# Routing without a sort: rows go to each expert's next place in DRAM, and answers come back by groups

## The chip, the cores and the metric

The kernel runs on one core of a Trainium2 chip. Its engines work side by side and wait for one another through semaphores: TensorE (PE in the profile; its weight loads are PEld), VectorE (DVE), ScalarE (ACT), GpSimd (POOL) and SyncE (SP). Every engine runs its own instructions in order. DMAs are issued from the queues of SP, ACT and POOL and share the core's 16 DMA engines. The metric is device time in microseconds of one execution.

## The reference

A four-layer model over x of 2048 tokens (2 x 1024) and 256 columns. Each layer adds a gated cross attention to a small context (64 rows a batch) and a gated feed-forward part to x. What matters here:

- Layer 0's feed-forward part is a mixture of 8 experts, two for each token, of hidden size 1024, with a capacity.
- Layer 1's feed-forward part has causal self-attention (16 heads of 16, 4 key heads) and then a mixture of 8 experts of hidden size 512, one for each token:

```python
x = x + out @ Wo + bo
h2 = rmsnorm(x, ln2_w)
logits = h2 @ Wr + br
top1 = jnp.argmax(logits, axis=-1).reshape(-1)
u = jnp.einsum('td,edf->tef', xt, W1) + b1
u1, u2 = (u[..., :HID], u[..., HID:])
act = u1 * jax.nn.sigmoid(u2)
y_all = jnp.einsum('teh,ehd->ted', act, W2) + b2
y = jnp.take_along_axis(y_all, top1[:, None, None], axis=1)[:, 0, :]
return x + y.reshape(batch, seq, DIM)
```

- Layer 2 is cross attention and a quantised product, layer 3 cross attention and a mixture of 16 experts. They are not changed, but layer 2's cross attention is the first reader of layer 1's answers.

## The kernel before, in words

The 2048 tokens are 16 row tiles of 128 (`NT`), four to a group of 512 (`NG` = 4 groups). x stays in SBUF for the whole run. TensorE's order is written out by hand (`manual_schedule`); on the other engines, and on the DMA queues, a planner orders the work at build time by its own estimates, and the chip then keeps that order.

*Layer 0's end* (`l0`). Each expert's rows are gathered from DRAM, worked on, and its answers scattered into `ybuf` (`scattered`, L1395, on POOL). When all are written (`wrote`), eight loads of 512 KB (L844, on SP, four buffers) bring them back, and 32 VectorE operations (L854) add them to x, for all four groups. Layer 1 begins after that.

*Cross attention* (`ctx_attn`, shared by layers 1 and 2). It works through the 16 row tiles. `norm` of a group (statistics on VectorE, the reciprocal root on POOL, scaling on ACT), `turn` and `project` give a group's queries. `norm(0)` and `norm(1)` stand before the loop, `norm(2)` and `norm(3)` in its steps 2 and 6. Layer 1's projection and norms for its self-attention (`l1_front`) run in the same loop as `then` steps.

*Self-attention* (`l1_attention`). For each of 16 query tiles: `scores`, exponentials and `values` in blocks, with the maxima for a tile two ahead (`greatest`); `place` writes the maxima into the queries by a POOL DMA (`qT<-mT`, L1210). Finished tiles queue their routing steps in `routing`: the gate (L1281), the output projection (L1290), `normed` (L1308, which also writes the normalised row to `hbuf` through SP, L1309), `turned` and `chosen` (L1325, the logits and the choice, a one-hot `oh`). They are queued four tiles at a time, so the last four tiles' steps run after the loop.

*Layer 1's experts* (`l1_experts`, L1552). All eight experts' weights are loaded by SP (L1564, L1568: 8 MB and 4 MB) into two tiles, while `sort_tiles` (L1429) turns the one-hots into a list for each tile of 128 rows of one expert: which rows to gather (`gi`), where their answers go (`si`) and which expert it is (`ei`). There are up to 23 tiles (`NS`); 19 always run, the last four under an `If`. For each tile POOL gathers the rows (`xg`, L1580) and the expert's biases spread over 128 partitions (`bt`, L1586, 640 KB), TensorE transposes the rows, multiplies (`up`, L1613, in two halves, `down`, L1633) with weights picked by a register, VectorE adds the biases (L1617, L1638), and POOL scatters the answers to the tokens' places. When all are written, four loads (L1670) bring them back and 16 operations add them to x (L236). Layer 2 begins after that, its loads behind these on SP.

## Time and profile before

| | us |
|---|---|
| median of 7 runs (2180.38 to 2190.69) | 2187.36 |
| the profiled execution | 2188.95 |
| its span | 2187.2 |
| busy: PE / DVE / ACT / POOL | 1849.0 / 1115.5 / 840.0 / 425.7 |
| layer 0's last answer on VectorE, first projection of layer 1 | 395.9, 428.8 |
| attention's last matmul, first matmul of the expert tiles | 981.5, 1032.1 |
| last answer of layer 1's experts, first projection of layer 2 | 1163.6, 1195.9 |

The profile is one execution. Its times start at the first instruction. A busy share says how long an engine worked in a stretch and not what held it when it did not; for that the view of the chain names what ended last at each step ("SPq" is the SP queue issuing a DMA, "issue" is time in which nothing that the profile shows was waited for). The granted clock is TensorE's as the throttle left it, 1.00 being full. In the timeline the start of a pipelined matmul is firm and its end modelled, so a step is read from start to start.

### The profile page before, as it was taken

The numbers are of one execution on the slowest core, as the hardware profiler recorded it, in microseconds if no ns is written. First come the engines' busy times: TensorE is split into PE (matmuls) and PEld (weight loads), VectorE is DVE, ScalarE is ACT, GpSimd is POOL, SyncE is SP. The second block draws the span as 40 slices with busy tenths as digits, with TensorE's granted clock in tenths as the row PEclk, the third lists the DMA queues.
The fourth block names the chain that finished last, engine by engine and source line by source line (L and its number), as shares of the span: only waits on it lengthen the run. The fifth ranks groups of instructions, "written<-read, shape, count | busy, mean of one in ns | idle before, by whom it ended". The sixth has DMA issues, their size and how long they took to land.

```text
span 2187.2 us, 26241 instructions
## 1 busy us (share of the span) xinstructions
PE 1849.0 (85%) x9627; PEld 1165.9 (53%) x9627; DVE 1115.5 (51%) x2437; ACT 840.0 (38%) x1603; POOL 425.7 (19%) x652
## 2 busy tenths in 40 slices
PE   7849999599778998993894978799999899998884
PEld 3437777377545455542553664455555555555563
DVE  5660010556677647722345763356662466655434
ACT  3402222354434564571112653354442454441121
POOL 1013331201421031113332133000000000000462
PEclk8969999799889999996997978799999999998997
DMA  4032331300000000006432200000000000002224
GB/s 145 20 110 88 118 118 62 115 1 1 7 2 2 1 11 2 11 11 252 158 141 84 97 1 0 0 1 1 1 1 0 1 1 1 1 1 87 61 89 155
DMA packets 70603, 107.09 MB, mean 49 GB/s; under 512 B 13779, under 2 KB 55382, under 8 KB 70214
## 3 DMA queue, kind: packets, MB, share of 16 engines
q1 hardware_dynamic: 54582, 63.17, 8.7%
q0 software_dynamic: 13824, 40.55, 5.5%
q8 instruction: 81, 1.33, 0.2%
q10 hardware_dynamic: 2064, 1.62, 0.2%
q14 instruction: 52, 0.43, 0.1%
HBM read 80.90 MB, written 24.15 MB: 48 GB/s over the span
## 4 chain that ended last, share of the span: by engine, by line
PE 49%; DVE 10%; issue 6%; ACT 6%; POOL 5%; DMA 3%; SPq 2%; another core or an unknown queue 0%; ACTq 0%; POOLq 0%; DVEq 0%
PE s L1910 6%; PE et L1933 4%; PE po L1945 4%; PE s L1174 3%; PE po L1244 3%; PE prj L204 3%; PE sT L1225 3%; PE po L352 3%; DVE nm L1180 2%; DVE nm L1918 2%; PE h L2084 1%; PE v L1840 1%; SPq L1568 1%; PE wo L2012 1%; PE s L548 1%
## 5 line engine op out<-in xcount | busy, mean ns | idle before, releaser
L1180 DVE TENSOR_REDUCE nm<-s 128x1 f32<-128x512 f32 (+3 forms) x304 | 184.0, 655 | 68.6 <-PE s L1179 46.7
L1920 ACT ACTIVATE e<-s,nm 128x1024 f32<-128x1024 f32 x128 | 141.4, 1110 | 180.2 <-DVE nm L1919 104.0
L1918 DVE TENSOR_REDUCE nm<-s 128x1 f32<-128x1024 f32 x128 | 150.9, 1219 | 97.6 <-PE s L1910 97.6
L1233 ACT ACTIVATE eT<-sT 128x512 f32<-128x512 f32 x288 | 148.8, 603 | 112.3 <-PE sT L1225 81.4
L1910 PE MATMUL s<-kT,qT 64*128 64x512 f32 x512 | 162.0, 635 | 11.1 <-ACT e L1920 11.1
L1933 PE MATMUL et<-ident,e 128*128 128x128 f32 x1024 | 140.8, 285 | 16.7 <-DVE eT L112 12.4
L1174 PE MATMUL s<-kT,qT 128*128 128x512 f32 (+3 forms) x384 | 129.4, 417 | 16.4 <-ACT qT L114 9.6
L1933 PEld LDWEIGHTS et<-ident,e 128*128 128x128 f32 x1024 | 114.4, 144 | 53.6 <-issue 22.2
L1945 PE MATMUL po<-eT,v 128*64 128x256 f32 x1024 | 125.6, 385 | 0.3 <-DVE eT L112 0.2
L1174 PEld LDWEIGHTS s<-kT,qT 128*128 128x128 f32 x384 | 73.1, 196 | 81.7 <-DVE nm L1180 27.1
L783 PE MATMUL h<-xeT,w 128*128 128x384 f32 (+1 forms) x416 | 108.9, 420 | 0.6 <-PEq L836 0.3
L112 DVE COPY eT<-et 128x512 f32<-128x512 f32 x128 | 87.8, 686 | 41.9 <-PE et L1933 39.9
L1945 PEld LDWEIGHTS po<-eT,v 128*64 128x64 f32 x1024 | 68.5, 136 | 69.4 <-issue 32.3
L787 ACT ACTIVATE hT<-h,b 128x384 f32<-128x384 f32 (+1 forms) x104 | 52.6, 508 | 137.5 <-PE h L783 120.8
L1957 POOL TENSOR_TENSOR ec<-scs,nm 128x1024 f32<-128x1024 f32 x8 | 15.2, 1901 | 461.4 <-DVE nm L1919 415.5
L793 DVE TENSOR_TENSOR y<-yp,b 128x256 f32<-128x256 f32 (+1 forms) x34 | 14.4, 422 | 177.3 <-PE yp L801 176.7
L801 PE MATMUL yp<-w,hT 128*128 128x256 f32 x464 | 102.8, 380 | 0.0
L1225 PE MATMUL sT<-qT,kT 128*128 128x512 f32 x288 | 96.9, 451 | 2.1 <-DMA qT<-mT 2.1
L1910 PEld LDWEIGHTS s<-kT,qT 64*128 64x128 f32 x512 | 58.5, 189 | 71.8 <-ACT e L1920 35.8
L801 PEld LDWEIGHTS yp<-w,hT 128*128 128x128 f32 x464 | 87.7, 190 | 15.5 <-issue 2.1
L1613 PE MATMUL up<-w,xT 128*128 x152 | 77.2, 632 | 15.2 <-DMA w<-in_L_ffn_W_dram 7.3
L783 PEld LDWEIGHTS h<-xeT,w 128*128 128x128 f32 x416 | 70.5, 191 | 35.4 <-issue 3.4
(495 smaller groups left out, 3580.1 us busy)
## 6 DMA issues: line engine op xcount, KB each, us to landing
w<-in_L_ffn_W_dram SPq DMA_DIRECT2D x24, 1024.0 KB
y<-ybuf SPq DMA_DIRECT2D x20, 512.0 KB
ybuf<-zero POOLq DMA_DIRECT2D x8, 512.0 KB
hbuf<-xn SPq DMA_DIRECT2D x32, 128.0 KB
w<-in_L_ffn_W_dram SPq DMA_DIRECT2D x8, 512.0 KB
x<-in_x_dram SPq DMA_DIRECT2D x16, 128.0 KB
hbuf<-hn SPq DMA_DIRECT2D x16, 128.0 KB
L_ffn_w1T<-in_L_ffn_w1T_dram SPq DMA_DIRECT2D x1, 2048.0 KB
```

The lines of the kernel that those rows point to most:

```text
L112: self.nc.vector.tensor_copy(out, in_)
L783: nc.tensor.matmul(p[:, :m], W[e][0][:, k, ts(hc, P)], X[e][:, k, r : r + m], start=k == 0, stop=k == DC - 1,)
L801: nc.tensor.matmul(p[:m, :D], hT[:, hc, r : r + m], W[e][1][:, hc, :], start=hc == 0, stop=hc == HC - 1,)
L1174: nc.tensor.matmul(o, qT[:, h0 + j, :], kT[:, (h0 + j) // 4, b * S + k0 : b * S + k0 + m], start=True, stop=k0 + m < n,)
L1180: nc.vector.tensor_reduce(nm[:, u, h0 : h0 + nh], s[:, : nh * m].rearrange("p (h k) -> p h k", h=nh), AX.X, ALU.max, negate=True,)
L1225: nc.tensor.matmul(s, kT[:, kv, b * S + kt * P : b * S + (kt + 1) * P], qT[:, 4 * kv : 4 * kv + 4, :], start=True, stop=kt < qt,)
L1233: nc.scalar.activation(eT[:, kv, :], s, AF.Exp)
L1910: nc.tensor.matmul(s[h][:, ts(u, 512)], qT[r, c, ts(2 * g + t, P)], kT[r, c, ts(u, 512)], start=True, stop=True,)
L1918: nc.vector.tensor_reduce(m, s[h], AX.X, ALU.max, negate=True)
L1920: nc.scalar.activation(e[n][h], s[h], AF.Exp, bias=m, accum_out=q["rs"][:, t, j])
L1933: nc.tensor.transpose(p[:, ts(j, P)], e[n][h][:, ts(k + j, P)], self.ident)
L1945: nc.tensor.matmul(po[j][64 * h : 64 * h + 64, :256], v[:, k, ts(2 * c + h, D3X)], eT[j][h][:, k, :], start=k == 0, stop=k == KM - 1,)
```

## The change

- Layer 1's sort goes. Every expert owns T rows of a DRAM buffer `xs1`. While attention still runs, `sent` counts a routed group's one-hots (two small matmuls), keeps a running row number for each expert in `bases`, and scatters each normalised row (POOL) to its expert's next row. The buffer's 17.8 MB are cleared beforehand: 68 DMAs of 256 KB on SP, five to a step of layer 1's cross attention.
- Routing is queued in groups of 4, 4, 4, 2, 1 and 1 row tiles; in the last two query tiles two steps are taken at a time, and a step waits until its tile's output has been turned.
- A tile of 128 rows is now a plain block of `xs1`. `tile_table` computes each tile's expert and first row; registers read from the table address three SP loads for each tile: its rows, its expert's W1 (1 MB) and its W2 (512 KB), four buffers each, three tiles ahead.
- Biases enter as matmuls: all experts' biases lie split into three bf16 parts in `bias1`, and a one-hot column `sel` of the tile's expert picks them (`biased`).
- A tile's answers overwrite its block (a POOL DMA with a register address). A token's answer is gathered by its row number (`slot`).
- The answers of layers 0 and 1 are no longer taken at the layer's end: `take(g)` is called by the next cross attention ahead of `norm(g)`. Layer 1's and layer 2's cross-attention pools release space tile by tile.

The diff, cut:

```diff
+NS1 = NT + E1 - 1
+R1 = T * E1 + 8 * P
     def ctx_attn(..., some=None, then=(), take=None):
-        qT, norm, turn, project = queries
+        qT, ready, turn, project = queries
+        def norm(g):
+            take(g)
+            ready(g)
     def l1_xattn(self, then, scratch, take):
-        with self.tc.tile_pool(name="l1x", bufs=1) as pool:
+        with self.tc.tile_pool(name="l1x", bufs=1, reuse_waits="tile") as pool:
...
             kbd, vblk = self.ctx_kv(pool, wk, wv)
+            scratch(pool)
     def l0(self, back):
-            for g in range(NG):
-                for u in range(2):
-                    y4 = pool.tile([P, 4, D], F32, tag="y4", name="y4", bufs=4)
+        def take(g):
+            for u in range(2):
+                y4 = back.tile([P, 4, D], F32, tag="y4", name="y4", bufs=2)
...
     def l1(self, take, taken, back):
+            def scratch(q):
+                row = q.tile([E1, 2 * H1 + D], F32, tag="brow1", name="brow1")
+                self.nc.sync.dma_start(out=row, in_=self.a["L1_ffn_b12"])
+                self.bias_rows(None, row, 2 * H1 + D, None, E1, d["bias"])
+                zero = q.tile([P, 512], F32, tag="zero1", name="zero1")
+                self.nc.gpsimd.memset(zero, 0.0)
+                flat = d["x"].rearrange("r d -> (r d)").rearrange("(k p f) -> k p f", p=P, f=512)
+                clear.extend(
+                    partial(self.nc.sync.dma_start, out=flat[k], in_=zero) for k in range(flat.shape[0])
+                )
+            def cleared(i):
+                if i > 0:
+                    for _ in range(5):
+                        if clear:
+                            self.after(clear.pop()(), self.first[-1:])
...
     def l1_attention(self, u, front, rest, front_done, ln2, d):
+            def sent(i, n):
+                v = nc.vector
+                q = oh[i].rearrange("p i e -> p (i e)")
+                m = n * E1
+                p = self.ps("count")
+                nc.tensor.matmul(p[:, m : 2 * m], self.ones, q, start=True, stop=True)
+                nc.tensor.matmul(p[:, :m], upper, q, start=True, stop=True)
+                within = p[:, :m].rearrange("p (i e) -> p i e", e=E1)
+                total = p[:, m : 2 * m].rearrange("p (i e) -> p i e", e=E1)
+                v.tensor_copy(bases[:, 0, :], bases[:, 4, :])
+                for j in range(n):
+                    o = bases[:, j + 1 if j + 1 < n else 4, :] if i + n < NT else d["next"]
+                    v.tensor_tensor(o, bases[:, j, :], total[:, j, :], ALU.add)
+                at = ap.tile([P, n, E1], F32, tag=f"at{n}", name="at")
+                v.tensor_tensor(at, within, bases[:, :n, :], ALU.add)
+                v.tensor_tensor(at, at, oh[i], ALU.mult)
+                row = ap.tile([P, 4], F32, tag="row", name="row", bufs=2)[:, :n]
+                v.tensor_reduce(row, at, AX.X, ALU.add)
+                v.tensor_copy(d["slot"][:, i : i + n], row)
+                for j in range(n):
+                    self.scattered(d["x"][:, :], d["slot"][:, i + j : i + j + 1], hn[i + j], d["put"])
...
+            few = {3: 4, 7: 4, 11: 4, 13: 2, 14: 1, 15: 1}
...
-                        if routing and (not tail or len(routing) > 9):
-                            routing.pop(0)()
+                        for _ in range(1 + (i > 13)):
+                            if routing and routing[0][0] in turned_back and (not tail or len(routing) > 9):
+                                routing.pop(0)[1]()
     def l1_experts(self, ln2, d, way):
+            self.tile_table(pool, d["next"], table, used)
+            sel = pool.tile([P, NS], BF16, tag="sel", name="sel")
+            nc.vector.tensor_scalar(sel, table[:, :, 0], d["p32"], None, ALU.is_equal)
...
+            def gather(s):
+                e = nc.values_load(table[0:1, s, 0:1], engines=[E.SP], min_val=0, max_val=E1 - 1)
+                r = nc.values_load(table[0:1, s, 1:2], engines=[E.SP, E.Pool], min_val=0, max_val=R1 - P)
+                xg = pool.tile([P, D], F32, tag="xg", name="xg", bufs=4)
+                ins = nc.sync.dma_start(out=xg, in_=d["x"][bass.ds(r, P), :])
+                own(ins.ins, wrote)
+                self.after(ins, d["put"])
+                read.append(ins.ins)
+                w1 = pool.tile([P, DC, 2 * H1], F32, tag="w1", name="w1", bufs=4)
                 nc.sync.dma_start(
+                    out=w1, in_=a["L1_ffn_W1"][bass.ds(e, 1)].rearrange("e (k p) h -> p (e k) h", p=P)
+                )
+                w2 = pool.tile([P, FC, D], F32, tag="w2", name="w2", bufs=4)
...
+            def biased(s, out, cols):
+                nc.tensor.matmul(
+                    out, sel[:, s : s + 1].to_broadcast([P, P]), d["bias"][:, cols], start=True, stop=False
+                )
             def up(s, w):
-                    reg[s] = nc.tensor.value_load(ei[0:1, s : s + 1], min_val=0, max_val=E1 - 1)
...
+                biased(s, p[:, h], h)
                 for k in range(DC):
+                    nc.tensor.matmul(p[:, h], xT[s][:, k, :], w1[:, k, h], start=False, stop=k == DC - 1)
-                nc.vector.tensor_tensor(u[:, h], p[:, h], bt[:, h], ALU.add)
                 if w:
-                    nc.scalar.activation(u[:, h], u[:, h], AF.Sigmoid)
+                    nc.scalar.activation(u[:, h], p[:, h], AF.Sigmoid)
                 else:
-                    nc.vector.tensor_tensor(u[:, h], u[:, h], u[:, H1:], ALU.mult)
+                    nc.vector.tensor_tensor(u[:, h], p[:, h], u[:, H1:], ALU.mult)
...
-                nc.vector.tensor_tensor(yo, y[:, :D], G[s][2][:, 2 * H1 :], ALU.add)
-                self.scattered(ybuf[:, :], si[:, s : s + 1], yo, wrote)
+                nc.vector.tensor_copy(yo, y[:, :D])
+                ins = nc.gpsimd.dma_start(out=ybuf[bass.ds(r, P), :], in_=yo).ins
+                own(ins, wrote + read)
+                wrote.append(ins)
...
+        def take(g):
+            for i in range(4 * g, 4 * g + 4):
+                y = way.tile([P, D], F32, tag="back", name="back", bufs=8)
                 self.after(
+                    nc.gpsimd.indirect_dma_start(
+                        out=y, out_offset=None, in_=ybuf[:, :],
+                        in_offset=bass.IndirectOffsetOnAxis(ap=slot[:, i : i + 1], axis=0),
                     ),
                     wrote,
                 )
+                self.add_gated(i, y, 5)
```

## The prediction, made before the result was known

> **What bounds the kernel now.** I read three views in this order: busy time by stretch, to find the stages in which TensorE is not full; the chain that ended last, to see what those stretches wait for; and the timeline of one expert tile, to see what TensorE pays for a tile.
>
> Busy time by stretch (start and end, length, busy time of PE, PEld, DVE, ACT and POOL with instruction counts, granted clock, DMA share, GB/s):
>
> ```profile
> 395.00:420.00 25.00, 0.40 (x2) 0.00 (x0) 16.30 (x45) 10.76 (x12) 3.96 (x10) 0.57 0.74 217
> 420.00:435.00 15.00, 12.50 (x36) 7.62 (x38) 12.76 (x49) 6.28 (x13) 8.38 (x14) 0.69 0.13 38
> ...
> 940.00:982.00 42.00, 41.42 (x246) 19.97 (x242) 5.14 (x15) 35.40 (x76) 9.64 (x16) 1.00 0.04 14
> 982.00:1005.00 23.00, 14.24 (x56) 9.83 (x57) 5.67 (x19) 6.70 (x18) 9.68 (x21) 0.80 0.07 23
> 1005.00:1032.00 27.00, 2.22 (x22) 1.43 (x21) 10.71 (x53) 0.00 (x0) 8.69 (x9) 0.50 1.01 396
> ...
> 1049.00:1164.00 115.00, 107.76 (x392) 64.81 (x392) 47.13 (x86) 20.80 (x36) 43.62 (x45) 1.00 0.34 121
> 1164.00:1196.00 32.00, 6.36 (x27) 5.46 (x27) 19.80 (x64) 3.98 (x9) 6.78 (x13) 0.57 0.44 130
> ```
>
> TensorE is full in the attention loop (41.42 of 42 us) and nearly so over the expert tiles (107.76 of 115). It is empty in three gaps: after layer 0's experts (395 to 420), between routing and layer 1's experts (1005 to 1032, all 16 DMA engines full) and after those experts (1164 to 1196).
>
> The chain in order of time (start, length, what), over the last two gaps:
>
> ```profile
> 979.54 1.98 PE po L1244 x16
> ...
> 984.83 2.00 PE gate L1281 x4
> ...
> 999.92 3.17 PE lg L1325 x14
> ...
> 1018.77 8.81 SPq L1568
> ...
> 1039.34 9.31 DMA w<-in_L_ffn_W_dram
> ...
> 1049.11 1.97 PE y L1633 x8
> ...
> 1143.17 24.63 DMA bt<-in_L_ffn_b_dram,ei
> 1168.16 3.81 DMA y<-ybuf
> 1171.99 3.27 DVE x L236 x8
> ...
> 1177.18 6.17 DMA mi<-in_mask_dram
> ```
>
> Attention ends at 981.5, routing of the last four row tiles at 1004.4; then the load of all eight experts' weights carries the chain until 1049. Behind the experts, the answers' way through DRAM and layer 2's own loads, queued behind it on SP, carry it.
>
> One tile's TensorE work:
>
> ```profile
> 1070.21 1.88 PE L1613 MATMUL up<-w,xT 128*128 x4
> 1071.92 0.60 PE L1626 MATMUL at<-ident,ub 128*128 128x128 f32 x4
> 1072.88 1.98 PE L1613 MATMUL up<-w,xT 128*128 x4 [0.35 <-DVE ub L1617]
> 1074.70 0.38 PE L1597 MATMUL xt<-ident,xg 128*128 128x128 f32 x2
> 1074.91 1.89 PE L1633 MATMUL y<-w,aT 128*128 x8
> ```
>
> The next tile's first row starts at 1076.64: 6.43 us a tile, of which TensorE waits 0.35.
>
> **The change, part by part.** The sum is made against the profiled execution, 2188.95 us (span 2187.2 and 1.75 around it). That is 1.59 above the median of 2187.36, which I take off at the end.
>
> *Layer 0's answers by groups: -10.* Now VectorE's last answer is ready at 395.86, the last scatter has landed at 399.53 (the release of POOL's brow memset), eight loads of y go out from 398.77, 32 adds to x run until 417.26, and only then the norms that feed TensorE's first projection, at 428.83. After, two loads and eight adds stand before the first norm. But on SP's queue the loads that layer 1 needs now come first in the program; those into the right-hand pools cannot go before 399.53. Some 12 issues at 0.45 each put the first y load at 405, with 1.6 MB of weights ahead of its 1 MB; at the 217 to 313 GB/s of this stretch y lands by 410.5. Adds end at 412.3, statistics at 412.9, POOL's rsqrt and mean take 2.3 (as from 420.57 to 422.91), ACT's four scalings 2.07, transposes and copies 1.2: first projection at 418.5. If y went first the gain would be 16; if VectorE is held by the new bias split or SP is later still, 4. I take 10, by the row of 0.45 an issue.
>
> *Layer 1's cross attention carries more: +3.* 24 adds of 0.40 to 0.48 (11 us) move beside a stage where VectorE is busy 106.76 of 165.6 us: 0 if they fit, 11 if all stall; I take 1. 68 clears of 256 KB write 17.8 MB; layer 0's zeros wrote at 406 GB/s, so 44 us of a DMA that is idle here (share 0.01). 68 SP issues at 0.45 are 31 us of an empty queue; behind them wait the y loads of group 3, with three row tiles of slack. The split of the eight experts' biases is three casts and two subtractions of 1280 columns: scaled from 0.35 and 0.53 at 384 columns, about 7 us of VectorE, most of it while VectorE waits for y: I take 2, ends 0 and 7.
>
> *Attention loop: +6.* Rows are now routed in groups of 4, 4, 4, 2, 1, 1, so three tiles' routing moves from the tail into a loop where TensorE is full: gate 1.3, output projection 2.9 (0.98 a tile), transposes 1.3, logits 0.6: 6.1; the counting matmuls of `sent` add about 0.3 for each of six groups. 8 us, less some 2 of gaps. On POOL each group's scatters (1.0 each) and on VectorE its ten 0.2 us operations stand before `qT<-mT`, which TensorE waits for only 2.1 us in all now; the cover is a query tile of lead. If it fails at each group, six times 2 us.
>
> *From attention to the first expert tile: -25.5.* Now 981.54 to the first up matmul at 1032.11: 50.6. After, step by step for one row tile: to the gate 3.3 (981.54 to 984.83); gate 1.9; projection, residual and square 2.6; POOL 1.5 and 0.6; transposes, copies and logits 1.8; choice 1.6 (six of 0.2 with gaps); count 1.4 (as 1004.42 to 1005.80); place 1.2: the scatter starts near 997.4 and has landed 3.9 us later (as 1164.25 to 1168.16). Beside it the tile table, 21 VectorE operations, takes 4 us at 0.19 each. Then two register reads on SP, xg, 1 MB of W1 at the 409 GB/s of this load: 2.6 plus about 2 from issue to landing: 1006.5, 25 us after attention. Register reads by an engine have no row of their own; TensorE's read for each tile leaves no gap in the 6.43, and POOL's first gather starts 0.83 after its index is written: 0 to 0.83 each, I take 0.5. The page "DMA: Bandwidth & Descriptors" of the Trainium skill (Latency and other measured facts) gives a floor of about 0.6 us for a `tensor_load`, which I read as such a register read; by it the pair on SP would cost 1.2, and no run here shows it.
>
> *The expert tiles: +7.* Now from 1032.11 to the last answer at 1163.97: 131.9, with the first tiles stalled on W2. Each tile gains three bias matmuls, 512, 512 and 256 columns of bf16; two 512-column bias matmuls of cross attention take 0.43 in the chain, so 0.54 a tile: 6.97. VectorE loses a 0.69 add, which gives nothing, as the half-tile wait then stands behind ACT's 0.63 sigmoid. 19 tiles are 132.4; the first 8 us at clock 0.50 (1032 to 1040 now) cost 4, the last tile's end 2: 138.4. The page "TensorE: Matmul & The Clock Gate" (Part 1) says that about 3.4 us of sustained work lift the clock; by it the cold start would cost 1.7 instead of 4. The trace's 8 us decides. Each tile now also loads 1.57 MB of weights and 0.13 of rows and writes 0.13: 1.83 MB, 4.5 us at 409 GB/s and 5.2 at the 349 of the W2 stretch, under the 6.97 that hides it, with three tiles of prefetch. The cost of this term runs from -3 (bias matmuls in the 0.35 wait and a short cold start) to +15 (a stall of 0.4 a tile).
>
> *Layer 1's answers by groups: -12.4.* Now 32 us from the last answer (1163.55) to the first projection (1195.91), among it 16 adds, the mask's load and its 2 us on VectorE. After: the write lands 4.6 later as now; four indirect gathers at POOL's pace of 1.25 with 3.0 from the last issue to data: 11.4; add and statistics 1.1; POOL's rsqrt stands behind group 1's four gathers: 16.5; scalings, transposes, copies 3.5: 20. If POOL does the rsqrt first, 2 less; if mask and weights are not in by then, 5 more.
>
> Sum: -10 + 3 + 6 - 25.5 + 7 - 12.4 = -31.9: 2157.0, or **2156** against the median.
>
> **The rivals.**
> *The queues give the answers back* (2173). SP sends layer 1's loads ahead of y and POOL holds the norms: the first boundary gains 0, the third 5: 17 us less gain. For it: both queues run in order and y now stands last on SP. Against: eight loads and 32 adds become two and eight.
> *Attention pays* (2168). The six groups each delay `qT<-mT` by 2 us on POOL. For: POOL's waits are in order; against: POOL is busy 9.64 of 42 us.
> *Larger gain* (2142). y first (6 more), bias matmuls half hidden in the 0.35 wait and a shorter cold start (8 more).
> *Slower: the tile loop is bound by its loads* (2214 at 10 us a tile, 19 times 3.03 over 2156). Place: SP, two register reads and three loads a tile, waiting for buffers. It decides at 8.6 us a tile, where 19 times 1.65 eat the 31.9, that is at 213 GB/s. For it: W1 and W2 are fetched 19 times instead of 8, with 1 KB rows in W2. Against: 349 to 414 GB/s in the present load, from the same queue.
>
> **How the numbers follow.** Forecast 0.50, with its own range 2145 to 2168; queues 0.17, attention pays 0.08, larger gain 0.12, load-bound 0.13. The measurement tells 0.2% (4.4 us) from no change. The first, second, third and larger cases are faster, 0.87, less 0.03 for their upper ends; of the load-bound case 0.01 falls within 0.2%: faster 0.84, same 0.04, slower 0.12. The range 2134 to 2188 holds all but most of the load-bound case and the low end of the larger gain.
>
> **What would show it.** Right: first projection of layer 1 near 418, first up matmul 25 us after attention's last matmul, tiles at 7.0 us with clock 1.00 and DMA share near 0.7, first projection of layer 2 20 us after the last answer. Wrong: tiles over 8 us with `up` waiting for w1 or w2 (slower), `sT` waiting for `qT<-mT`, or y landing after 415.

## The result, and the profile after

The changed kernel takes 2203.01 us (median of 19 runs, 2194.22 to 2209.26), and the kernel before, run beside it, 2185.47 (median of 46 runs, 2173.63 to 2194.35). The ratio is 1.0073 with a 95% interval of 1.0061 to 1.0085: the change costs 16 us where the prediction saw a gain of 31. The profiled execution took 2205.66, its span 2204.0.

The two traces are compared by five stages, each from one mark to the next, so that what came earlier does not count. "Answers" are the starts of VectorE's last `y` of layer 0 and last `yo` of layer 1's tiles. The `qkv` products and attention end with the modelled end of their last matmul (`po` for attention); the tiles begin with the first `up<-w`, layer 3 with its first projection.

| stage, us | before | after | forecast | change seen | change forecast |
|---|---|---|---|---|---|
| last answer of layer 0 to end of the `qkv` products | 198.4 | 199.2 | 191.4 | +0.8 | -10 + 3 |
| attention, to the last `po` | 387.6 | 418.1 | 393.6 | +30.5 | +6 |
| to the first up matmul | 50.7 | 30.0 | 25.2 | -20.7 | -25.5 |
| expert tiles, to the last answer | 131.4 | 135.2 | 138.4 | +3.8 | +7 |
| last answer of layer 1 to layer 3 | 152.5 | 158.3 | 140.1 | +5.8 | -12.4 |
| sum | 920.6 | 940.8 | 888.7 | +20.2 | -31.9 |

What lies outside was not changed and still differs between executions: layer 0 ends at 395.44 before and at 400.52 after, and from layer 3's first projection to the end it takes 871.2 and 862.8. In the twelve kernels below the same two pieces lie between 390.0 and 400.4 and between 839 and 864. So a stage of a profile is compared with the same stage, and a time only as a ratio to the kernel before on the same chip.

Busy time by stretch of the changed kernel (start and end, length, busy time of PE, PEld, DVE, ACT and POOL with instruction counts, granted clock, DMA share, GB/s):

```profile
395.00:420.00 25.00, 10.94 (x42) 8.71 (x40) 10.19 (x31) 10.85 (x12) 5.32 (x13) 0.73 0.46 126
420.00:440.00 20.00, 5.80 (x14) 3.07 (x15) 18.41 (x47) 4.73 (x9) 4.14 (x8) 0.57 0.37 115
...
945.00:985.00 40.00, 33.85 (x167) 18.32 (x167) 7.96 (x30) 23.67 (x54) 14.43 (x21) 0.87 0.05 20
985.00:1018.00 33.00, 27.12 (x141) 13.49 (x137) 5.93 (x31) 18.39 (x42) 9.44 (x15) 0.84 0.02 9
1018.00:1048.00 30.00, 8.03 (x29) 5.19 (x30) 9.46 (x48) 4.43 (x11) 6.51 (x13) 0.57 0.30 98
1060.00:1180.00 120.00, 115.53 (x449) 70.57 (x447) 25.52 (x53) 19.37 (x36) 9.28 (x17) 1.00 0.69 233
1180.00:1217.00 37.00, 11.11 (x38) 7.69 (x36) 19.96 (x63) 5.99 (x12) 24.41 (x30) 0.63 0.37 104
```

Attention is no longer full: 33.85 of 40 us and 27.12 of 33, at clocks of 0.87 and 0.84, where the kernel before had 41.42 of 42 at 1.00. The gap of 27 us with full DMA engines that the kernel before had ahead of its tiles is gone (DMA share 0.30 from 1018 to 1048). Over the tiles TensorE is busy for 115.53 of 120 us; it waits there 0.25 a tile, for ACT, and for no load. The two stretches behind the answers are still mostly empty (5.80 of 20 us and 11.11 of 37).

TensorE's waits from 920 to 1020 in the changed kernel (what it waited for, total, times, longest):

```profile
PE tr L190 <- POOL hn L1359: 6.6, 4, 2.5
PE count L1389 <- DVE oh L253: 2.1, 2, 1.4
PE wo L1343 <- DVE oT L1337: 2.1, 2, 1.4
...
PE lg L1374 <- ACT hT L1366: 0.3, 1, 0.3
```

All four are steps of the routing, 11.1 us together. In the kernel before, TensorE waits once from 920 to its last `po`, for 1.0.

From the chain that ended last (start, length, what), at the first and at the second boundary:

```profile
406.98 2.17 SPq L127
410.73 4.22 DMA row<-in_bias_rows_dram
...
1198.06 3.01 POOL back L1791
```

Behind the answers of layer 0 the chain runs over `WkT` and `row`, loads of layer 1 on SP, and then over VectorE's own operations until group 0's adds are done; behind those of layer 1 it runs over POOL's gathers, one of which took 3.01.

### The profile page after: what moved, and what is told of

Its sections match the earlier page's. It is cut to its first block, busy times and chain, and to the rows that moved or that the text cites. A ratio compares the mean times of both kernels' runs of the same rounds, so it can differ in the third digit from the quotient of the medians.

```text
span 2204.0 us, 26615 instructions
## 1 busy us (share of the span) xinstructions
PE 1868.1 (85%) x9696; PEld 1176.5 (53%) x9696; DVE 1097.8 (50%) x2433; ACT 841.3 (38%) x1611; POOL 416.2 (19%) x657
## 4 chain that ended last, share of the span: by engine, by line
PE 49%; DVE 10%; issue 10%; ACT 6%; POOL 4%; DMA 3%; SPq 0%; POOLq 0%; another core or an unknown queue 0%; ACTq 0%; DVEq 0%
PE s L2035 6%; PE et L2058 4%; PE po L2070 4%; PE po L1296 3%; PE s L1226 3%; PE prj L206 3%; DVE nm L1232 3%; PE po L354 2%; PE h L2209 2%; PE sT L1277 2%; DVE nm L2043 2%; PE v L1965 1%; PE wo L2137 1%; PE s L556 1%; PE et L577 1%
## 5 line engine op out<-in xcount | busy, mean ns | idle before, releaser
L1285 ACT ACTIVATE eT<-sT 128x512 f32<-128x512 f32 x288 | 149.2, 603 | 128.6 <-PE sT L1277 92.2
L2058 PE MATMUL et<-ident,e 128*128 128x128 f32 x1024 | 138.4, 281 | 17.3 <-DVE eT L114 12.7
L1226 PE MATMUL s<-kT,qT 128*128 128x512 f32 (+3 forms) x384 | 131.1, 422 | 17.8 <-ACT qT L116 10.9
L116 ACT COPY eT<-et 128x512 f32<-128x512 f32 x128 | 71.8, 593 | 37.8 <-PE et L2058 37.5
```

The costliest lines, as they stand in the source:

```text
L1226: nc.tensor.matmul(o, qT[:, h0 + j, :], kT[:, (h0 + j) // 4, b * S + k0 : b * S + k0 + m], start=True, stop=k0 + m < n,)
L1285: nc.scalar.activation(eT[:, kv, :], s, AF.Exp)
L2058: nc.tensor.transpose(p[:, ts(j, P)], e[n][h][:, ts(k + j, P)], self.ident)
```

## The experiments

Each kernel was run beside the kernel before on the same chip, four or two kernels at a time; the kernel before took 2162.68, 2163.60, 2183.88 and 2158.96 in these four groups. My theory after reading the traces had three parts. *Exposed chains*: the routing steps stand in TensorE's hand-written order where no other work is left. *Queue order*: at both boundaries the data of group 0 is there, and an engine's or queue's order puts something else first. Against both stood *the added work*: counts, scatters, clears and biases cost what they cost, wherever they stand.

### Attention: the pairs of steps

The timeline of TensorE in the changed kernel, where group 8 to 11 is routed (start, length, line, operation; in brackets the idle time before and what ended it):

```profile
958.67 0.28 PE L1341 MATMUL wo<-borow,onesb 128*128 128x256 bf16 x1
...
960.74 1.19 PE L1277 MATMUL sT<-qT,kT 128*128 128x512 f32 x4
964.46 3.04 PE L190 MATMUL tr<-ident,hn 128*128 128x128 f32 x8 [2.53 <-POOL hn L1359]
...
968.17 3.16 PE L1374 MATMUL lg<-L_ffn_Wr,hT 128*128 128x8 f32 x14 [0.26 <-ACT hT L1366]
971.26 1.94 PE L1296 MATMUL po<-eT,v 128*32 128x512 f32 x8
```

The last output projection (958.67) and the norm are taken in the same block. The norm's transposes (`tr`) then need ACT's `y`, VectorE's sum, ACT's square and POOL's root and scaling, and they start 4.7 behind the projection's end (959.75). TensorE has 2.2 us of other work (`po` and `sT`) and stands for 2.53. Then it runs at half speed: the eight transposes take 3.04 (1.16 in the group before, at 924.07), the value matmuls 1.94 (1.07). The choice is taken in the same block as the transposes and waits again.

*Groups of four, one step a block* (e1_four):

```diff
-            few = {3: 4, 7: 4, 11: 4, 13: 2, 14: 1, 15: 1}
+            few = {3: 4, 7: 4, 11: 4, 15: 4}
-                        for _ in range(1 + (i > 13)):
+                        for _ in range(1):
-                    o = bases[:, j + 1 if j + 1 < n else 4, :] if i + n < NT else d["next"]
+                    o = d["next"] if i + j + 1 == NT else bases[:, j + 1 if j + 1 < n else 4, :]
```

The last line is needed because the changed kernel's form carries the row numbers on only if the last group is a single tile.

> Routing in groups of four again (the last one after the loop) and one routing step for each block of keys; counting, scatters, clears and everything else as in the changed kernel. Theory 'exposed chains': the attention loop lost its 30 us because two routing steps at a time were taken in the last two query tiles, where no maxima work is left to fill TensorE, so that each step waits for ACT, VectorE and POOL in turn. Then the last value matmul of the last query tile stands near 985 instead of 1016, the routing tail of four tiles takes 23 us plus 3 for the count, the first up matmul stands near 1030 instead of 1048, and the time is 2188 (2183 to 2194). Rival 'the added work': counts, scatters and clears slow the loop wherever they stand. Then the last value matmul stays near 1012 to 1016, the first up matmul goes to about 1062 and the time to 2220.

Measured: ratio 1.0017 (0.9990 to 1.0043), 12 us below the changed kernel. Attention takes 386.1 (before 387.6), from its end to the first up matmul 45.7; the last `po` starts at 982.89, the first up matmul at 1030.6. The counts and scatters of twelve of the 16 row tiles are in this loop and cost it nothing that can be seen; the clears lie ahead of it, in cross attention (452 to 548 in the changed kernel). The added work falls as the cause.

*The small groups, one step a block* (e2_single):

```diff
-                        for _ in range(1 + (i > 13)):
+                        for _ in range(1):
```

> The small groups of the change (4, 4, 4, 2, 1, 1), but one routing step for each block of keys. 17 steps are then left over for the time after the loop. Exposed chains, with the pairs of steps as the cause: the loop ends near 990, the left-over steps take about 28 us (4 for the rest of the group of two, 12 for each single tile, by the 12 us from gate to slot in the changed kernel's last group), the first up matmul stands near 1033 and the time is 2191. If the small groups cost by themselves, whoever takes them, the first up matmul stays at 1045 to 1050 and the time at 2203 to 2208. The added work: loop end near 1010, time 2215 or more.

Measured: ratio 1.0008 (0.9990 to 1.0026). Attention takes 394.2, then 43.8 to the first up matmul at 1039.3. Without the pairs of steps 23.9 of the 30.5 are gone from attention, and 13.8 come back as steps left over behind it. The loop ends 5.5 later than expected (995.5 against 990); the way from there is as expected (43.8 against 43). The times do not separate this kernel from the one with groups of four: the intervals overlap.

### The first boundary: what stands ahead of y

Queue entries and operations of the changed kernel at the boundary (timeline; SP, then DVE):

```profile
406.98 2.17 SPq L127 DMA_DIRECT2D L_xattn_WkT<-in_L_xattn_WkT_dram  x1
...
411.44 26.72 SPq L857 DMA_DIRECT2D y<-ybuf  x7
...
419.97 0.81 DVE L622 CAST bias<-brow 8x1280 bf16<-8x1280 f32 x1
420.71 0.47 DVE L867 SCALAR_TENSOR_TENSOR x<-y,keep,x 128x256 f32<-128x256 f32 x1
421.10 1.47 DVE L624 TENSOR_TENSOR brow<-brow,bias 8x1280 f32<-8x1280 f32 x1
422.50 0.47 DVE L867 SCALAR_TENSOR_TENSOR x<-y,keep,x 128x256 f32<-128x256 f32 x1
```

SP starts when layer 0's last scatter has landed (404.23, 3.7 behind the last answer), sends twelve loads of layer 1, among them one that takes 2.17 to issue, and comes to y at 411.44. VectorE meanwhile begins with layer 1's keys and values, and when it comes to x (420.71), it waits for no data, but the split of the eight experts' biases stands between the adds: 0.81, 1.47, 0.82, 1.48, 0.82, that is 5.4.

*Group 0 first* (e3_first): its answers are taken at the end of layer 0, ahead of layer 1 in the program.

```diff
-        return take
+        take(0)
+        return lambda g: take(g) if g else None
```

> The answers of group 0 alone are taken at the end of layer 0, so that its two y loads stand ahead of layer 1's twelve loads on SP; groups 1 to 3 as in the changed kernel. Theory 'queue order': the first boundary gained nothing since y stands behind those loads and the split of the biases stands between the adds. From the last answer to the first projection it then takes 20 to 25 us instead of 36, and the time falls by 10 to 15, to 2191 to 2196. Rival: the return of the answers takes as long by itself, or layer 1's weights are next in line. Then the first projection stays at 32 us or more and the time within 4 us of 2203.

Measured: ratio 1.0024 (1.0006 to 1.0042), 11 us below the changed kernel. First projection 20.1 behind the last answer (changed: 36.2), the whole stage 191.4 instead of 199.2:

```profile
399.14 0.92 SPq L857 DMA_DIRECT2D y<-ybuf  x2
...
403.23 3.25 DVE L867 SCALAR_TENSOR_TENSOR x<-y,keep,x 128x256 f32<-128x256 f32 x8 [5.75 <-DMA y<-ybuf]
...
415.94 3.70 PE L206 MATMUL prj<-xnT,L_xattn_WqT 128*128 128x512 f32 x8 [0.65 <-ACT xnT L333]
```

The same two loads, issued 3.3 behind the last answer instead of 10.9, and eight adds in 3.25 without a gap. Of the 16 gained at the first projection, 8 are left at the end of the stage. The bias split now stands before group 1's adds and the first maxima; in e6_all below, where it is moved as well, the stage is 3.4 shorter, so it is a part of what was given back. This edit moves y ahead on SP and on VectorE at once and does not part the two.

### The second boundary

The changed kernel behind the last answer of the tiles, at 1182.91 (timeline; SP, POOL, DVE):

```profile
1184.38 0.38 SPq L127 DMA_DIRECT2D L_xattn_WkT<-in_L_xattn_WkT_dram  x1
...
1186.68 1.04 POOL L1791 DMA_INDIRECT back<-xs,slot  x1 [2.52 <-issue]
...
1205.66 0.24 POOL L148 TENSOR_SCALAR r<-mv 128x4 f32<-128x4 f32 x1
...
1197.77 2.48 DVE L286 TENSOR_TENSOR kbd<-kT,bm 128x512 f32<-128x512 f32 x4
```

Group 0's gathers start at 1186.68 and its adds end at 1196.5. Its root on POOL starts 9 us later, at 1205.66: VectorE does layer 2's keys, values and mask first (1197.26 to 1203.4), whose loads SP sent only after the tiles, and POOL has thirteen gathers in front.

*Layer 2's loads early* (e4_prefetch):

```diff
                     if s + 3 < b:
                         G[s + 3] = gather(s + 3)
+                    if s == 6:
+                        self.loaded = self.l2_loads(way)
```

`l2_loads` holds the lines of `l2_xattn` from the weights' loads to `some`; the planner put them in front of the first tile.

> Layer 2's cross-attention weights, biases and mask are loaded ahead of the expert tiles, into space that lives through them; nothing else is moved. Theory 'late loads': at the second boundary VectorE works on layer 2's keys, values and mask between the adds and the statistics, because their loads come only after the last tile. With them early the reciprocal root of group 0 starts about 1198 minus 1183 = 15 us after the last answer instead of 22.7, the first projection follows at 24 to 26 instead of 33, and the time falls by 7 to 9, less up to 3 for 1.3 MB more ahead of the first expert's loads. Rival 'gathers': POOL's gathers of group 1 stand before the root and hold it. Then the first projection stays at 31 to 33 and the time does not fall.

Measured: ratio 1.0064 (1.0043 to 1.0085), within the interval of the changed kernel. First projection 30.7 instead of 33.4, the stage 155.1 instead of 158.3. The gathers hold it: with the keys out of the way, POOL's root still started behind thirteen of them, 20.3 behind the last answer.

*All together* (e6_all): routing in groups of 4, 4, 4, 2, 2, one step a block and one block left free behind `normed` and `chosen`; group 0 first; the bias split at step 8; layer 2's loads early; each group's gathers behind the root of the group before; the table's index rows made early.

```diff
+            few = {3: 4, 7: 4, 11: 4, 13: 2, 15: 2}
+                        if pause:
+                            pause = False
+                        elif routing and routing[0][0] in turned_back and (not tail or len(routing) > 9 or i > 8):
+                            f = routing.pop(0)[1]
+                            f()
+                            pause = i > 12 and f.func in (normed, chosen)
...
+                if i == 8:
+                    split.pop()()
...
-                    wrote,
+                    wrote + ([self.rooted] if g else []),
```

> Everything that the runs so far point to, in one kernel without the sort: routing in groups of 4, 4, 4, 2 and 2, one step a block, a block left free behind the norm and behind the choice, steps from query tile 9 on taken beside the tail of a tile; group 0 of layer 0's answers taken before layer 1's loads, the split of the biases moved to step 8 of cross attention; layer 2's loads ahead of the expert tiles, and POOL's gathers of groups 1 to 3 behind the root of the group before; the two index rows of the tile table made at layer 1's start. If the three losses (exposed chains, y behind the loads, gathers before the root) are what ate the gain, then: first projection of layer 1 20 us after the last answer; attention loop (that projection to the last value matmul) 565 to 575 against 550.6 of before and 579 of the change; first up matmul 36 to 40 after the last value matmul; tiles 135 to 136; first projection of layer 2 20 to 22 after the last answer; the time 25 to 32 below the kernel before, a ratio of 0.985 to 0.989. If chip-wide variation or the added work is the cause, the ratio stays above 0.995.

Measured: ratio 0.9947 (0.9926 to 0.9969), faster than the kernel before, by less than half of what was expected; the interval holds the 0.995 above which chip-wide variation or the added work was to be the cause, so that the stages have to decide. The first stage takes 188.0, attention 389.6, then 33.5, the tiles 134.8: these four are as expected or better. The first projection of layer 2 comes 18.0 behind the last answer, earlier than expected, but the stage takes 157.0, almost what it took in the changed kernel. VectorE waits in it (timeline of e6_all):

```profile
1164.14 0.48 DVE L238 SCALAR_TENSOR_TENSOR x<-back,tg,x 128x256 f32<-128x256 f32 x1 [5.27 <-DMA back<-xs,slot]
...
1192.58 0.48 DVE L238 SCALAR_TENSOR_TENSOR x<-back,tg,x 128x256 f32<-128x256 f32 x1 [5.51 <-DMA back<-xs,slot]
```

Three times (the third at 1175.36, after 5.64) it waits over 5 us for a gather that may go only behind the root of the group before, 16.4 in all.

*The same with groups of four* (e9_fourall; `few` and the single step as in e1_four).

> As the kernel with everything, but routing in groups of four, as in the kernel before, the last one after the loop. Exposed chains says that the small last group is worth 6 to 10 us when its steps are spread, so this kernel is slower than the other by that, a ratio of 0.989 to 0.993. If the loop cannot take any more work without a loss, the two are equal.

Measured: ratio 0.9981 (0.9962 to 1.0000), 7.3 us slower than e6_all by the ratios. Attention and the way to the first up matmul take 392.1 + 44.0 against 389.6 + 33.5: once its steps are spread, the small last group is worth 7 us by the ratios and 13 by these two stages, where 6 to 10 were expected.

*All answers at the layer's end* (e7_undo): the changed kernel with `take` called for every group at the end of layers 0 and 1.

```diff
-        return take
+        for g in range(NG):
+            take(g)
+        return lambda g: None
```

> The changed kernel, but all answers of layers 0 and 1 are taken at the layer's end, as before. Queue order says that taking them by groups, as written, gained next to nothing: the time stays within 5 of the changed kernel, a ratio of 1.005 to 1.010 to before. If it gained what the forecast said (10 and 12.4), this kernel is 20 us slower than the changed one, a ratio of 1.016.

Measured: ratio 1.0121 (1.0078 to 1.0164), an interval that holds both 1.010 and 1.016. The stages say 202.6 (changed: 199.2) and 160.1 (158.3): groups as written gained 5.2 over taking everything at the end in this kernel, and nothing over the kernel before, whose first stage, with four buffers for y and no bias split, is 198.4 and whose answers of layer 1 came back in four plain loads.

*Three gathers ahead* (e10_ahead) and *only group 0's root ahead* (e11_ahead0); both also read the number of tiles behind the tiles, load the Sigmoid table early and take the scaling of a bias of layer 2 out of the tile table.

```diff
-                    wrote + ([self.rooted] if g else []),
+                    wrote + ([self.roots[(i - 7) // 4]] if i >= 7 else []),
```

In e11_ahead0 the index of `self.roots` is 0. `i` counts the 128-row tiles of the answers, `roots[g]` is the POOL step of the norm of group g that the gather waits for.

> As the kernel with everything, with the second boundary and the start of the tiles changed. There each group's four gathers stood behind the root of the group before, so that VectorE waited 5.3, 5.6 and 5.5 for data that had only then been asked for, and the first projection's gain of 15 was given back before layer 3. Here three of a group's four gathers may go ahead of that root. Besides, the scaling of layer 2's bias no longer stands inside the tile table on VectorE (2.1), the Sigmoid table is loaded before the first tile (1.3), and the read of the number of tiles comes after the 19 tiles. Theory 'late requests': from the last answer to layer 3's first projection 146 to 152 instead of 157 (before: 152.5), first up matmul 32 to 34 after the last value matmul instead of 35.8, time 8 to 13 below that kernel, ratio 0.988 to 0.991. Rival: that stretch is held by VectorE's and ACT's own work for the 16 row tiles, not by the answers. Then it stays at 155 to 158 whatever comes first, and the time falls by 3 at most, ratio 0.993.

> The same, but only the root of group 0 is put ahead of the gathers, at the eighth; all others may go at once. Late requests: as good as the other or 1 to 3 better, since the data of groups 2 and 3 comes sooner. If POOL's roots of groups 1 and 2 behind eight gathers (10 us) hold TensorE, it is 3 to 6 slower than the other.

Measured: ratios 0.9901 (0.9878 to 0.9925) and 0.9897 (0.9870 to 0.9923); the stage takes 152.4 and 152.5, just above the expected 146 to 152 and 4.6 less than in e6_all: most of the three waits' 16.4 did not come back. The tiles take 132.5 and 132.4, 2.3 less. That is not shown to be the table: it is loaded early in e12_later and e13_adds too, and TensorE's wait behind the first up product falls from 2.01 to 0.73 in all four, but there the tiles take 134.5, with the second up product still at half speed (3.62 instead of 1.88). The first up matmul still comes 33.3 behind attention: the tile table, ready at 997.98, had not been the last thing; the last scatter of rows, issued at 996.78, was, and SP's `xg` went at 1002.20. With the first projection 14 us earlier than in the kernel before, the stage is as long as there. TensorE's waits and ACT in e11_ahead0 say why:

```profile
PE s L557 <- ACT qT L212: 8.1, 1, 8.1
```

```profile
1164.12 2.08 ACT L165 ACTIVATE xn<-x,m,r 128x256 f32<-128x256 f32 x4 [9.87 <-POOL m L161]
1166.10 0.67 ACT L212 ACTIVATE qT<-prj,bq 128x512 f32<-128x512 f32 x1
```

The queries of group 0 (`qT<-prj`) stand on ACT behind the scaling of group 1, which waits until 1164.1 for its root on POOL. TensorE has projected group 0 at 1158 and gets its queries at 1166.8.

*ACT's order* (e12_later) and *VectorE's order* (e13_adds):

```diff
         norm(0)
-        norm(1)
         with tc.manual_schedule(engines={mybir.EngineType.PE}):
             turn(0)
             project(0)
+            norm(1)
...
+                ins = self.scaled(xn[g][t], self.x[4 * g + t], r[:, t : t + 1], m[:, t : t + 1])
+                if g == 1:
+                    self.after(ins, [self.turned])
...
+                ins = self.add_gated(i, y, 5)
+                if g > 1:
+                    self.after(ins, [self.less[1 if g == 2 else 4]])
```

The last three lines are in e13_adds alone.

`turned` is ACT's last copy of a projection, `less` the subtraction of a tile's maximum on VectorE. e12_later keeps e11_ahead0's gathers, e13_adds has e10_ahead's.

> As the kernel with only the root of group 0 ahead of the gathers, and the scaling of group 1 on ACT comes after group 0's queries in both cross attentions. In that kernel TensorE waited 8.1 for ACT's qT, which stood behind group 1's scaling, which waited for group 1's root on POOL behind eight gathers: the early first projection (18.6 after the last answer, 32.4 in the kernel before) was waiting there, so that layer 3's first projection came at 152.5, as before. Theory 'queues in order, one behind the other': the 8.1 falls to 1 or 2, but the first maximum on VectorE stands behind all sixteen adds and so comes only some 4 earlier; last answer to layer 3: 148 to 150; ratio 0.987 to 0.989. Rival 'paced by its own work': 152 to 153, ratio 0.990.

> The same, and VectorE's adds of groups 2 and 3 come after the first two and the first five tiles' maxima, and POOL's root of group 1 before the gathers of group 2. Queues in order: the first maximum follows the first scores at once, some 9 earlier than in the kernel with only the root of group 0 ahead; last answer to layer 3: 143 to 147; ratio 0.984 to 0.987. If the next queue takes it back (group 1's scaling, its projection, the roots of groups 2 and 3), it stays at 148 to 151.

Measured: ratios 0.9892 (0.9868 to 0.9916) and 0.9849 (0.9823 to 0.9875); the stage takes 149.2 and 140.1. For e12_later that is as expected, for e13_adds 3 better. The 9.1 between the two belong to two edits, the adds and the gathers; the gathers alone made no difference between e10_ahead and e11_ahead0. The wait for `qT` is gone in both; in the second the scores follow the projection and the maxima the scores:

```profile
1163.91 4.96 PE L206 MATMUL prj<-xnT,L_xattn_WqT 128*128 128x512 f32 x8
1168.70 0.60 PE L695 MATMUL s<-mask,ident 128*128 128x512 bf16 x2
1169.23 1.14 PE L559 MATMUL s<-kbd,qT 64*128 64x256 f32 x8
...
1170.41 1.22 DVE L568 TENSOR_REDUCE mx<-s 128x16 f32<-128x1024 f32 x1 [5.52 <-PE s L559]
```

140.1 is what the prediction had for this stage (152.5 less 12.4), but it took the order of POOL, ACT and VectorE to get there, which that term did not hold. e13_adds is the fastest kernel of the study, 1.5% below the kernel before, where the prediction had 1.4%; its five stages sum to 890.2, against 920.6 before and the forecast's 888.7. That these two lie so close is in part chance: the way to the first up matmul takes 9.9 more than forecast, and three other stages together 8.4 less.

### The bias matmuls

e8_nobias leaves the three bias matmuls of a tile out, and with them the experts' biases:

```diff
-                biased(s, p[:, h], h)
-                biased(s, y[:, :D], slice(2 * H1, HB))
```

> The changed kernel without the three bias matmuls of a tile (layer 1's expert biases are left out). If they stand on TensorE's path, a tile takes 6.2 to 6.3 instead of 6.75 and the 19 tiles 10 us less. If they are hidden, or the loads set the pace, the tile stays at 6.6 to 6.75.

Measured in its one run: 6.33 a tile and 127.8 for the stage, against 6.77 and 135.2. The bias matmuls stand on TensorE's path, at 0.44 a tile and 7.4 for the stage. One tile of the changed kernel on TensorE:

```profile
1101.35 0.38 PE L1712 MATMUL up<-bias,sel 128*128 128x512 bf16 x1 [0.25 <-ACT ub L1737]
1101.56 1.88 PE L1735 MATMUL up<-w,xT 128*128 128x512 f32 x4
...
1103.49 0.27 PE L1712 MATMUL y<-bias,sel 128*128 128x256 bf16 x1
1103.60 1.89 PE L1753 MATMUL y<-w,aT 128*128 128x256 f32 x8
1105.33 0.38 PE L1712 MATMUL up<-bias,sel 128*128 128x512 bf16 x1
1105.55 1.88 PE L1735 MATMUL up<-w,xT 128*128 128x512 f32 x4
```

Three starts of bias matmuls to the next matmul: 0.21, 0.11 and 0.22, 0.54 as forecast. Leaving them out saves 0.1 less, because the up product behind the wait then takes 1.98 instead of 1.88. And without them the tile is 0.1 shorter than in the kernel before (6.43), since the add on VectorE is gone and the half-tile wait is 0.25 instead of 0.35. That leaves 0.34. The rival of tiles bound by their loads is excluded with it: without the biases the same loads fit in 6.33.

## Why the prediction was wrong, point by point

The forecast and the stages lie 52.1 apart. Three steps of the prediction failed: the attention loop's cost (24.5), the wait behind layer 1's answers (18.2) and the one behind layer 0's (7.8). The way to the first tile adds 4.8, and the tiles give 3.2 back.

- *Layer 0's answers, -10, and cross attention, +3.* +0.8 instead of -7. The queue was nearly right: "Some 12 issues at 0.45 each put the first y load at 405", 9.6 behind the start of the last answer, and it went at 411.44, 10.9 behind it. The step that failed is "Adds end at 412.3", which has VectorE take y as it lands. VectorE was on layer 1's keys, values and bias rows until 420, and group 0's adds ran from 420.7 to 428.9. The bias split was given "I take 2, ends 0 and 7"; it measured 5.4, in the worst place. The gain itself is real: 191.4 with group 0 first, 188.0 with the split moved as well, that is 10.4 below before. The clears hurt nobody: from first projection to the end of the stage it is 163.0 after and 165.0 before.
- *Attention, +6.* +30.5. The step that failed is "8 us, less some 2 of gaps": it summed the engines' work and looked for the cover of `qT<-mT`, for which TensorE waited 2.1 in all, as before. What was not read is TensorE's own order: two dependent steps with 2.2 us of other work between them, when the chain from one to the next over ACT, VectorE and POOL took 4.7. Of the 30.5, TensorE is idle for 12.8 (51.8 against 39.1 us over the stage), 11.1 of them in the routing's four waits, and busy for 17.7 (366.2 against 348.6). Of the busy time an estimate gives 8.7 to the lower clock (0.13 of 33.85 and 0.16 of 27.12 us busy), which leaves 9.0 for the moved work, near the 8 of the sum. With spread steps the term is +2 (e6_all) to +5 (e10_ahead).
- *Attention to the first tile, -25.5.* Right in kind, -20.7 in size. The steps up to the scatter are met: scatter 15.6 behind attention, forecast 15.9. Then the table started 1.3 late, since its index rows were made on POOL behind the scatter (1034.43); SP needed 1.6 from the table to its first load instead of 0.5; W1 landed 6.8 behind its issue instead of 4.6, with the next tiles' loads sent behind it.

```profile
1034.43 0.18 POOL L1498 IOTA iai<- 128x23 int32 x1
...
1038.58 0.19 DVE L1664 CAST table<-ef 128x46 int32<-128x46 f32 x1
...
1040.36 0.35 SPq L1695 DMA_DIRECT2D xg<-xs  x1
1040.92 0.39 SPq L1700 DMA_DIRECT2D w<-in_L_ffn_W_dram  x1
...
1047.75 3.75 PE L1735 MATMUL up<-w,xT 128*128 128x512 f32 x4 [4.19 <-DMA w<-in_L_ffn_W_dram]
```

  "Register reads by an engine have no row of their own" was a misreading: the trace has each as a `TENSOR_LOAD`, 0.30 on TensorE in the kernel before (L1608). SP's two reads of the table take 0.27 each here, and each stands 0.57 ahead of what follows, so the pair cost 1.14 where the prediction set 0.5. The page "DMA: Bandwidth & Descriptors" of the Trainium skill (Latency and other measured facts) gives a floor of about 0.6 us for a `tensor_load`; the 0.57 agrees with it, the 0.27 of the read itself is less.
- *The tiles, +7.* +3.8: 0.34 a tile instead of 0.54, for the reasons above, 5.8 over seventeen tiles; the first answer stands 17.2 behind the first up matmul, 1.8 less than before. The load-bound rival, the only one on the slower side, did not occur.
- *Layer 1's answers, -12.4.* "POOL's rsqrt stands behind group 1's four gathers: 16.5" assumed that only they stand there; it was thirteen, and VectorE's keys and mask besides: 22.7 (20.3 in e4_prefetch, with the thirteen alone). "If mask and weights are not in by then, 5 more" was the right worry with too small a weight. The larger error was the end point. The term was read at the first projection, and e6_all to e11_ahead0 show that projection 14 us earlier than in the kernel before with the stage as long as there or longer (152.4 to 157.0 against 152.5), because POOL's root, ACT's queries and VectorE's adds each had the next thing in front.
- *The rivals.* "The queues give the answers back" and "attention pays" both happened, at once, with 26.0 and 24.5 us instead of 17 and 12. They were given 0.17 and 0.08 as alternatives, so that no case held their sum, and that sum is the sign of the result. The mechanism of the second was another one than named: TensorE's order, not POOL's delay of `qT`.

## What to carry to other kernels

A gain at the first instruction behind a wait is worth what is left of it at the end of the stage: follow the data one group further, through each engine's and queue's fixed order, before it is booked. Where steps of a latency chain are put into a hand-written order, count the other work between two of them against the chain's length, and add what a low clock does to the work behind each stall. And rivals that can happen together need a case in which they do.

## What the runs showed of the hardware

- A stall of TensorE of 2.53 us cost more behind it than in it. Stretches of the changed kernel around it (clock in the third column from the end):

```profile
955.00:962.00 7.00, 6.93 (x39) 3.52 (x37) 1.46 (x3) 6.00 (x16) 0.00 (x0) 1.00 0.02 4
...
964.40:968.00 3.60, 3.17 (x10) 1.98 (x10) 0.00 (x0) 1.05 (x2) 3.60 (x8) 0.50 0.00 0
968.00:971.00 3.00, 2.83 (x14) 2.83 (x14) 0.00 (x0) 0.12 (x1) 3.00 (x5) 0.50 0.00 0
971.00:975.00 4.00, 4.00 (x18) 2.04 (x19) 1.14 (x6) 1.04 (x3) 0.12 (x1) 0.60 0.00 0
```

  From start to start, the transposes, the logits without their wait and the value matmuls behind it took 4.3 more than those of the group before (2.86, 3.68 and 1.87 against 1.30, 1.83 and 1.00). The page "TensorE: Matmul & The Clock Gate" of the Trainium skill (Part 1) has the clock fall after an idle window of about 3.4 us; here it fell after less. The length of the stall alone did not decide: after 1.81 us of waiting (at 986.2) the clock stayed at 1.00 until 995, and with 1.39 (at 994.9) it was 0.81 from 995 to 1000.
- From a cold start the clock did not rise after a fixed time. In e10_ahead the first up matmul of the tiles starts at 1007.92, and the clock was 0.50 from 1007 to 1010, 0.70 to 1012 and 1.00 from then on, so it rose some 3.3 us behind it. In e12_later that matmul starts at 1002.03, and the clock was 0.50 until 1011 and 0.99 from 1011 to 1016, some 9 us behind, with the same wait of 0.73 between the first two up products. What sets the moment is not shown.
- A gather of 128 rows had its data 5.1 us after the issue in the changed kernel (1186.68), beside layer 2's loads, and 3.0 in e6_all (issued at 1150.01, added at 1153.03), where these had been loaded early. In a row of four there the adds follow one another in 1.1 to 1.4 us, and POOL issues one in 1.25 to 1.5. Four groups' answers are sixteen gathers, some 20 us of POOL by this pace, where the kernel before had four plain loads.
